# Bringing a column block back from DRAM as two half loads, each issued behind the next half block's store

## The chip, the cores and the metric

The kernel runs on one core of a Trainium2 chip. The metric is the device time of one execution in microseconds. Three runs of the kernel before took 485.42, 486.91 and 487.61 us; their median is 486.91 us. The profile shows one further execution.

## The reference

The reference is a graph layer followed by a mixture of eight experts, on 2048 nodes of 256 features. Cut to what matters:

```python
row, col = src, dst                       # 67584 edges, sorted by dst
gathered = edge_weight[:, None] * layernorm(x)[col]
x = x + segment_sum(gathered, row, num_segments=2048) + node_vec1
# experts, on x after a second layer norm xn:
top_p, top_idx = top_k(softmax(xn_in @ Wr + br), 2)
y_e = gelu((xn * ln_g[e] + ln_b[e]) @ W1[e] + b1[e]) @ W2[e] + b2[e]
x = x + weighted sum of the two chosen y_e
```

Only the first half is touched by the change: the sum over edges, which the kernel turns into a product of a 2048 x 2048 matrix A (a row for each src, a column for each dst, the edge weight as its entry) with the normalised nodes.

## The kernel before, in words

**Building A.** The columns of A are built in 16 column blocks of 128 destinations, and each block in two halves of 64 columns, so there are 32 half blocks, n = 0 to 31 (`NH`, the loop at L513). For a half block VectorE makes three tiles of ones and zeros: `hl` (the low seven bits of src, L328), `eq` (the high bits and the column of a pair, L335) and `hr` (eq times the weight, in three bf16 parts, L343). TensorE multiplies them, 96 small matmuls in `make_cols` (L367), ScalarE copies the result from PSUM to the SBUF tile `ar` (L370, two copies), and SyncE's queue stores `ar` to a DRAM tile `ad` (L371, 512 KB in rows of 512 bytes). The store is a transposition: partition (j, b) of `ar` goes to row 8m + j of `ad`, so that a column of A is a row of `ad`. Half h of a block fills rows 64h to 64h + 63.

**Using A.** When both halves of block cb are stored, one load (L374, 1 MB) brings `ad` back as the tile `ac`, 128 columns on 128 partitions. `dense` (L376 to L385) multiplies a few column blocks (a group of `GROUPS`: blocks 0-2, 3-6, 7-10, 11-13, 14-15) by the normalised nodes `xn` for two of the sixteen row blocks; VectorE adds the result to `acc` (L388), or, up to n = 16, ScalarE stages it and GpSimd's queue adds it by DMA (L396).

**The order.** In this part of the program the order on every engine is written out by hand (`manual_schedule` with all engines). In step n VectorE makes the tiles of half block n + 1 while TensorE runs `make_cols(n)`; from n = 8 on a `dense` follows it: group 0 in n = 8 to 15, group 1 in n = 16 to 23, group 2 in n = 24 to 31, eight pairs of row blocks each. Every fourth half block needs a new window of 128 x 128 edges (GpSimd's indirect DMAs, L242), whose keys VectorE prepares and TensorE transposes (L309). After the loop the first five pairs of group 3 and one of group 4 follow (L599 to L603), then the rest of the dense work and the expert part.

**Queues and buffers.** SyncE's queue issues its DMAs in program order. A load of `ac` waits there until the stores that it reads have landed, and everything behind it in that queue waits too. The behind-lying instructions in step n are the stores of the next half blocks and, at n = 12, two stores of zeros (L588, L590); behind the last load are the experts' weights (L988 to L991). `ar` has three buffers (`rowsp`), `hr` and `hl` two each, `ad` four; the tiles `ac` lie in two pools (`cols_0` with three buffers, `cols_1` with five), so that block 11 takes the buffer of block 3, which the last `dense` of group 1 frees.

Of the kernel before, what the change touches and what calls it, by code (L numbers as in the profile page):

```python
# [22 lines left out]
P = 128  # L23
# [4 lines left out]
def kernel(  # L28
# [30 lines left out]
    nc = tc.nc  # L59
# [170 lines left out]
    def count_before(q):  # L230
        sign = find.tile([P, RUN_0], BF16, name="sign")
        nc.scalar.activation(sign[:, :runs[q].shape[1]], runs[q], AF.Sign, bias=colp[:, q:q + 1],
                             scale=-1.0, accum_out=at[:, q:q + 1])
# [44 lines left out]
    def keys_of(q):  # L278
        b_i, f = low_key(q)
        nc.vector.tensor_tensor(f[:, 1, :], cls[q], b_i, OP.add)  # L280
        return f
# [33 lines left out]
    def next_part(q, i):  # L315

        k2, w2, rest = parts[q]
        r = prep.tile([P, P], F32, name=f"r{i}")
        nc.vector.tensor_tensor(r, rest, w2[:, :, i - 1, 0], OP.subtract)
        nc.scalar.copy(w2[:, :, i, :], r[:, :, None].to_broadcast([P, P, 2]))  # L320
        parts[q] = (k2, w2, r)

    def make_hl(n, hl=None, m=slice(0, GH)):


        k2, g = parts[n // 4][0], n % 4
        hl = hotl.tile([P, GH, P], BF16, name="hl") if hl is None else hl
        nc.vector.tensor_tensor(hl.rearrange("p g (n t) -> p g n t", t=2)[:, m],  # L328
                                two(k2[:, 0], g, P)[:, m], pair(P)[:, m], OP.is_equal)
        return hl  # L330

    def make_eq(n):
        k2, g = parts[n // 4][0], n % 4
        eq = hotr.tile([P, GH, RK], BF16, name="eq")
        nc.vector.tensor_tensor(eq.rearrange("p g (n t) -> p g n t", t=2),  # L335
                                two(k2[:, 1], g, RK), pair(RK), OP.is_equal)
        return eq

    def make_hr(n, eq):
        w2, g = parts[n // 4][1], n % 4  # L340
        hr = hotr.tile([P, GH, 3, RK], BF16, name="hr")
        w = w2[:, g * GH:(g + 1) * GH].rearrange("p g i t -> p (g i) t")
        nc.vector.tensor_tensor(  # L343
            hr.rearrange("p g i (n t) -> p (g i) n t", t=2),
            eq[:, :, None, :].to_broadcast([P, GH, 3, RK]),
            w[:, :, None, :].to_broadcast([P, GH * 3, RK // 2, 2]), OP.mult)
        return hr
# [5 lines left out]
    def make_cols(n, hl, hr):  # L353


        cb, h = n // 2, n % 2
        if h == 0:
            ads[cb] = dram.tile([P, NB, P], F32, name="ad", bufs=CB)
        ad_v = ads[cb].rearrange("(m j) b r -> (j b) m r", m=GB // QP)
        ar = rowsp.tile([P, GH // QP, P], F32, name="ar")  # L360
        for m0 in range(0, GH // QP, 4):
            pa = ps_a.tile([P, 4, P], F32, name="pa")
            for m in range(4):
                for i in range(3):
                    for j in range(QP):
                        g = (m0 + m) * QP + j
                        nc.tensor.matmul(pa[j * RK:(j + 1) * RK, m, :], hr[:, g, i, :],  # L367
                                         hl[:, g, :], start=(i == 0), stop=(i == 2),
                                         tile_position=(0, j * RK))
            nc.scalar.copy(ar[:, m0:m0 + 4, :], pa)  # L370
        nc.sync.dma_start(ad_v[:, h * GH // QP:(h + 1) * GH // QP, :], ar)  # L371
        if h == 1:
            acs[cb] = (cols_0 if cb in GROUPS[0] or 8 <= cb < 11 else cols_1).tile([P, NB, P], F32, name="ac")
            nc.sync.dma_start(acs[cb], ads[cb])  # L374

    def dense(blocks, b, between={}):  # L376

# [9 lines left out]
    def add(b, pa):  # L387
        nc.vector.tensor_add(acc[:, b:b + 2, :], acc[:, b:b + 2, :], pa[:, :, :DX])  # L388
# [9 lines left out]
    ads, acs = {}, {}  # L398
    ET = mybir.EngineType
    ALL = {ET.DVE, ET.Pool, ET.PE, ET.Activation, ET.SP}  # L400
    with tc.manual_schedule(engines=ALL):
# [8 lines left out]
        def center_router():  # L410
            nc.vector.memset(wc[:, :, NE:], 1.0)
            nc.vector.scalar_tensor_tensor(
                wc[:, :, :NE], tr[:, None, nt:nt + NE].to_broadcast([P, KD, NE]), -1.0 / D, wr_sb,
                op0=OP.mult, op1=OP.add)
# [90 lines left out]
        NH = 2 * NB  # L505
# [7 lines left out]
        for n in range(NH):  # L513
            q = n // 4
            f = None
            new = q + 1 if n > 4 and n % 4 == 2 and q + 1 < GQ else None
            if n + 1 < NH:
                hl = make_hl(n + 1) if n else hl_1
                if n == 1:
                    center_router()  # L520
                if n == 3:
                    next_part(1, 2)
                if n == 2:
                    fq = 1
                    f = keys_of(1)
                if new is not None:
                    next_part(new, 1)
                hots[n + 1] = hl, make_hr(n + 1, make_eq(n + 1))
                if new is not None:
                    next_part(new, 2)  # L530
            if n % 4 == 0 and q + 2 < GQ:
                count_before(q + 2)
            if n % 4 == 0 and q and q + 1 < GQ:
                fq = q + 1
                f = keys_of(fq)
            elif n % 4 == 1 and q + 2 < GQ:
                get_win(q + 2)
                if q + 4 < GQ:
                    get_run(q + 4)
            if n in (5, 8, 11, 14):  # L540
                b = 4 * (n // 3 - 1)
                scales_x(slice(b, b + 4))
            if n in (7, 10, 12, 14):
                b = {7: 0, 10: 4, 12: 8, 14: 12}[n]
                weigh_n(slice(b, b + 4))
            for p in late:
                (add_apart if n <= NB else add)(*p)
            late = []
            make_cols(n, *hots.pop(n))
            g, k = divmod(n - NB // 2, NB // 2)  # L550
            if g >= 0:
                late.append(dense(GROUPS[g], 2 * k))
            if n == 0:

                tr = ps_k.tile([P, 3, P], F32, name="pk").rearrange("p a b -> p (a b)")
                nt = NE * KH + 2 * NE * KD + NB
                cols = consts.tile([P, nt], F32, name="cols")
                o = 0
                for rows in (b1_rows, g_rows, be_rows, nv_rows):
                    m = rows.shape[0]  # L560
                    nc.tensor.transpose(tr[:, o:o + m], rows, ident[:m, :m])
                    o += m
                for k in range(KD):
                    nc.tensor.matmul(tr[:, nt:nt + NE], ones, wr_sb[:, k, :], start=(k == 0),
                                     stop=(k == KD - 1))
                nc.scalar.copy(cols, tr[:, :nt])
                nv_c = cols[:, NE * (KH + 2 * KD):]
            if n % 4 == 3 and q + 2 < GQ:
                scale_dst(q + 2)
            if 1 <= n < 9:  # L570
                weigh_x(n - 1)
            if n < 8:
                turn_x(n)
            if n == 1:
                scale_dst(1)
                sort_cols()
            if f is not None:
                turn_keys(fq, f)
            if n == 2:
                next_part(1, 1)  # L580
            for m, work, j in X_WORK:
                if m == n:
                    work(j)
            if n == 12:

                less_m = small.tile([P, NB], F32, name="less_m", bufs=1)
                nc.vector.tensor_tensor(less_m, less, nv_c, OP.subtract)
                nc.sync.dma_start(xr_d[N:, :].rearrange("(t p) c -> p t c", p=P),  # L588
                                  none[:, None, :].to_broadcast([P, TT, RW]))
                nc.sync.dma_start(y_d[N:, :].rearrange("(t p) d -> p t d", p=P),  # L590
                                  none[:, None, :D].to_broadcast([P, TT, D]))
            if n == NH - 3:
                used = small.tile([P, 1], F32, name="used", bufs=1)
                nc.vector.tensor_reduce(used, used_q, AX.X, OP.add)
                used_i = small.tile([1, 1], I32, name="used_i", bufs=1)
                pu = ps_k.tile([P, 3, P], F32, name="pk")[:, 0, :1]
                nc.tensor.matmul(pu, ones, used, start=True, stop=True)
                nc.vector.tensor_copy(used_i, pu[0:1, :])
        for p in range(NA // 2):  # L599
            late.append(dense(GROUPS[3], 2 * p))  # L600
            add(*late.pop(0))
# [722 lines left out]
```

## Time and profile before

| | |
|---|---|
| median of three runs | 486.91 us |
| the profiled execution | 489.3 us |
| its span on the core | 487.4 us |
| TensorE busy, share of the span | 446.5 us, 92% |
| VectorE busy | 268.8 us, 55% |
| stores `ad` | 32 of 512 KB, 6.8 us from issue to landing (median) |
| loads `ac` | 16 of 1024 KB, 6.1 us from issue to landing (median) |
| mean granted TensorE clock | 0.978 |

The edge part lies in the first 192 us of the span or so; the loads `ac` are issued from 29.4 to 193.4 us. VectorE's busy share over the whole kernel says little: in the forty slices of the page it is nine tenths or more from the second slice to the twelfth, which is most of the edge part, and low after it. A time in the working below is a start in the span unless it is called a duration. "Landing" is the time at which a DMA's semaphore says that all of its data are there.

### The profile page before, as it was taken

To read this page: it belongs to the slowest core of one execution; us is meant where nothing else is said; L and a number is where in the kernel's file an instruction comes from. 1 tells how busy PE (TensorE), PEld (TensorE's weight loads), DVE (VectorE), ACT (ScalarE), POOL (GpSimd) and SP (SyncE) were. 2 spreads that over 40 slices of the span, in tenths; PEclk is the share of its full clock that TensorE was granted. 3 is DMA by queue.
4 is the path that set the end of the run, shared out by engine and by line. 5 is a ranking of instruction groups with operands and counts; after the bars stand their busy time and mean duration, and the time that the engine had idled before them with its cause. 6 is when DMAs were issued, how large, how long until landed. Compare 5 with 4: busy or idle time off the path is not lost. (4 is left out here: it accounts for less than half of the span.)

```text
span 487.4 us, 12242 instructions
## 1 busy us (share of the span) xinstructions
PE 446.5 (92%) x5040; PEld 384.1 (79%) x5040; DVE 268.8 (55%) x558; ACT 199.3 (41%) x496; POOL 174.3 (36%) x141
## 2 busy tenths in 40 slices
PE   1588898889996999999999999999999999999895
PEld 0477787667885888888988888888888888879784
DVE  5999999999997975248772312334333212210011
ACT  2568759652432211056772233332334332324320
POOL 5561636653220000002744433554343444222223
PEclk9987799999998999999999999999999999999999
DMA  3678769998768866994629997899999676642331
GB/s 99 235 186 243 232 183 265 265 234 227 198 192 244 254 192 186 344 373 138 122 86 270 323 272 220 223 350 365 354 325 287 183 223 196 174 103 26 100 130 43
DMA packets 88372, 105.58 MB, mean 217 GB/s; under 512 B 9920, under 2 KB 77616, under 8 KB 86192
## 3 DMA queue, kind: packets, MB, share of 16 engines
q1 hardware_dynamic: 79072, 88.95, 58.1%
q0 software_dynamic: 9200, 15.67, 14.4%
q8 instruction: 44, 0.72, 0.6%
q14 instruction: 24, 0.20, 0.1%
q10 hardware_dynamic: 32, 0.04, 0.0%
HBM read 75.11 MB, written 29.47 MB: 215 GB/s over the span
## 5 line engine op out<-in xcount | busy, mean ns | idle before, releaser
L1115 PE MATMUL py<-w,hT 128*128 128x256 f32 x544 | 120.4, 380 | 0.0
L1068 PE MATMUL ph<-xeT,w 128*128 128x256 f32 (+1 forms) x544 | 115.1, 368 | 3.1 <-PEq L1278 1.3
L1070 ACT ACTIVATE hT<-ph,ec 128x256 f32<-128x256 f32 (+1 forms) x136 | 61.9, 460 | 123.9 <-PE ph L1068 69.7
L1115 PEld LDWEIGHTS py<-w,hT 128*128 128x128 f32 x544 | 102.4, 191 | 13.0
L1068 PEld LDWEIGHTS ph<-xeT,w 128*128 128x128 f32 x544 | 98.1, 191 | 16.5 <-issue 3.0
L383 PE MATMUL py<-xn_lo,ac 128*128 128x264 f32 x352 | 86.8, 399 | 5.6 <-DMA ac<-ad 5.6
L1123 POOL DMA_INDIRECT y_d<-ys,to_i x30 | 48.2, 1607 | 112.5 <-DVE ys L1118 80.2
L383 PEld LDWEIGHTS py<-xn_lo,ac 128*128 128x128 f32 x352 | 65.8, 193 | 18.9 <-DMA ac<-ad 6.4
L328 DVE TENSOR_TENSOR hl<-k,iota_b 128x4096 bf16<-128x4096 bf16 (+1 forms) x33 | 73.3, 2220 | 2.5 <-PE pa L367 1.4
L367 PE MATMUL pa<-hl,hr 128*32 128x128 bf16 x3072 | 56.2, 234 | 12.4 <-DVE hr L343 6.6
L367 PEld LDWEIGHTS <-hr 128*32 128x32 bf16 x3072 | 49.1, 104 | 22.6 <-issue 10.8
L1118 DVE SCALAR_TENSOR_TENSOR ys<-py,wt,b2w 128x256 f32<-128x256 f32 x34 | 16.3, 483 | 79.6 <-PE py L1115 76.4
L343 DVE TENSOR_TENSOR hr<-eq,w 128x3072 bf16<-128x3072 bf16 x32 | 56.3, 1758 | 1.9 <-DVE eq L335 0.5
L1042 DVE TENSOR_SCALAR xeT<-px,ec 128x256 f32<-128x256 f32 (+1 forms) x36 | 17.4, 525 | 64.5 <-PE px L1030 64.5
L370 ACT COPY ar<-pa 128x512 f32<-128x512 f32 x64 | 35.4, 593 | 39.0 <-PE pa L367 21.7
L995 POOL DMA_INDIRECT xs<-xr_d,to_i x32 | 33.4, 1045 | 15.2 <-DVE ys L1118 5.6
L242 POOL DMA_INDIRECT win_s<-in_src,at_i x8 | 15.9, 1989 | 60.3 <-DVE at_i L238 45.8
L383 PE MATMUL py<-xn_hi,ac 128*128 128x264 f32 x160 | 36.5, 388 | 0.3 <-PEq L613 0.3
L383 PEld LDWEIGHTS py<-xn_hi,ac 128*128 128x128 f32 x160 | 30.2, 190 | 5.6 <-PEq L613 0.7
L388 DVE TENSOR_TENSOR acc<-acc,py 128x528 f32<-128x528 f32 x29 | 20.3, 701 | 20.9 <-PE py L383 20.7
L1057 ACT ACTIVATE b2w<-b,wt 128x256 f32<-128x256 f32 x36 | 16.3, 500 | 25.7 <-DVE wt L1055 25.7
L335 DVE TENSOR_TENSOR eq<-k,iota_b 128x1024 bf16<-128x1024 bf16 x32 | 21.9, 684 | 0.0
(224 smaller groups left out, 358.7 us busy)
## 6 DMA issues: line engine op xcount, KB each, us to landing
w<-in_L_ffn_W SPq DMA_DIRECT2D x40, 1024.0 KB, 9.2
ad<-ar SPq DMA_DIRECT2D x32, 512.0 KB, 6.8
ac<-ad SPq DMA_DIRECT2D x16, 1024.0 KB, 6.1
b<-in_L_ffn_b SPq DMA_DIRECT2D x20, 128.0 KB, 9.2
acc<-st POOLq DMA_DIRECT2D x8, 264.0 KB, 8.0
acc<-in_x SPq DMA_DIRECT2D x4, 512.0 KB, 4.5
out<-y_d SPq DMA_DIRECT2D x4, 512.0 KB, 4.6
xr_d<-rec SPq DMA_DIRECT2D x1, 1300.0 KB
```

The costliest lines, as they stand in the source:

```text
L328: nc.vector.tensor_tensor(hl.rearrange("p g (n t) -> p g n t", t=2)[:, m], two(k2[:, 0], g, P)[:, m], pair(P)[:, m], OP.is_equal)
L335: nc.vector.tensor_tensor(eq.rearrange("p g (n t) -> p g n t", t=2), two(k2[:, 1], g, RK), pair(RK), OP.is_equal)
L343: nc.vector.tensor_tensor(hr.rearrange("p g i (n t) -> p (g i) n t", t=2), eq[:, :, None, :].to_broadcast([P, GH, 3, RK]), w[:, :, None, : ...
L367: nc.tensor.matmul(pa[j * RK:(j + 1) * RK, m, :], hr[:, g, i, :], hl[:, g, :], start=(i == 0), stop=(i == 2), tile_position=(0, j * RK))
L370: nc.scalar.copy(ar[:, m0:m0 + 4, :], pa)
L383: nc.tensor.matmul(pa[:, i, :DX], acs[c][:, b + i, :], xn(c), start=(c == blocks[0]), stop=(c == blocks[-1]))
L388: nc.vector.tensor_add(acc[:, b:b + 2, :], acc[:, b:b + 2, :], pa[:, :, :DX])
L995: nc.gpsimd.indirect_dma_start(out=(sets[s.set][0] if into is None else into)[:, t, cols], out_offset=None, in_=(xr_d if rows is None else ...
L1068: nc.tensor.matmul(ph, w1[:, k, c * P:(c + 1) * P], xeT[:, k, :], start=(k == 0), stop=(k == KD - 1))
L1070: nc.scalar.activation(hT[:, c, :s.n * P], ph, AF.Gelu, bias=ec[:, c:c + 1], scale=1.0)
L1115: nc.tensor.matmul(py, hT[:, c, t * P:(t + 1) * P], w2[:, c, :], start=(c == 0), stop=(c == KH - 1))
L1123: st = nc.gpsimd.indirect_dma_start(out=y_d[:, :], out_offset=bass.IndirectOffsetOnAxis(ap=tos[s.to][:, t:t + 1], axis=0), in_=ys, in_offs ...
```

## The change

The one load of a block becomes two, each of 64 of its rows onto 64 partitions (512 KB). A half load is no longer issued behind the store that it reads, but one half block later: at the end of `make_cols(n)`, behind the store of half block n, the half n - 1 is loaded. The last half is loaded after the loop. The buffer of `ac` is taken when the first half of a block is loaded, which is at the same place of the program where the whole block was loaded before.

```diff
         nc.sync.dma_start(ad_v[:, h * GH // QP:(h + 1) * GH // QP, :], ar)
-        if h == 1:
+        if n > 0:
+            get_half(n - 1)
+
+    def get_half(n):
+        cb, h = n // 2, n % 2
+        if h == 0:
             acs[cb] = (cols_0 if cb in GROUPS[0] or 8 <= cb < 11 else cols_1).tile([P, NB, P], F32, name="ac")
-            nc.sync.dma_start(acs[cb], ads[cb])
+        rows = slice(h * P // 2, (h + 1) * P // 2)
+        nc.sync.dma_start(acs[cb][rows], ads[cb][rows])
...
                 nc.vector.tensor_copy(used_i, pu[0:1, :])
+        get_half(NH - 1)
         for p in range(NA // 2):
             late.append(dense(GROUPS[3], 2 * p))
             add(*late.pop(0))
```

Nothing moves on TensorE, VectorE, ScalarE or GpSimd; SyncE's queue gets 16 more DMAs and the new order: store n, half load n - 1, store n + 1, half load n, and so on.

## The prediction

> **What bounds the kernel now.** I read the slices of the page first, then what SyncE's queue and TensorE wait for, then the timeline around each wait of TensorE. The slices:
>
> ```profile
> PE   1588898889996999999999999999999999999895
> DVE  5999999999997975248772312334333212210011
> PEclk9987799999998999999999999999999999999999
> DMA  3678769998768866994629997899999676642331
> ```
>
> VectorE is full up to slice 12 (146 us) and sets the pace at first; TensorE is full from slice 10 on, but for slice 13 (146 to 158 us), where its clock dips too. The waits of SyncE's queue over the span (total, times, longest):
>
> ```profile
> SPq L374 <- DMA ad<-ar: 98.2, 16, 15.4
> SPq L371 <- ACT ar L370: 51.9, 18, 11.2
> ```
>
> Each load sits about 6 us behind the store just ahead of it, and the next stores sit behind the load. TensorE's waits from 85 to 240 us, the three longest:
>
> ```profile
> PE py L383 <- DMA ac<-ad: 5.6, 2, 3.8
> PE pa L367 <- issue: 2.1, 1, 2.1
> PE pa L367 <- ACT ar L370: 0.6, 1, 0.6
> ```
>
> Where these fall, from the timeline (start, duration, engine, instruction; the brackets are the idle time ahead):
>
> ```profile
> 103.82 2.49 PE L383 MATMUL py<-xn_lo,ac 128*128 128x264 f32 x10 [1.76 <-DMA ac<-ad]
> 106.57 1.52 PE L367 MATMUL pa<-hl,hr 128*32 128x128 bf16 x96
> 112.58 1.08 ACT L370 COPY ar<-pa 128x512 f32<-128x512 f32 x2 [4.22 <-DMA ad<-ar]
> 140.61 1.76 DVE L343 TENSOR_TENSOR hr<-eq,w 128x3072 bf16<-128x3072 bf16 x1 [0.48 <-DVE eq L335]
> 144.86 0.33 SPq L374 DMA_DIRECT2D ac<-ad  x1
> 151.04 4.04 PE L383 MATMUL py<-xn_lo,ac 128*128 128x264 f32 x10 [3.84 <-DMA ac<-ad]
> 155.47 1.52 PE L367 MATMUL pa<-hl,hr 128*32 128x128 bf16 x96
> ```
>
> TensorE is without a gap from 103.82 to 147.2 us, except 0.58 us at 112.6; from 151.04 it is full to the end of the edge part and, with waits of about 3 us in all, through the experts to 470 us. So from 92 us on, what TensorE waits for is what the end waits for. (The 2.1 us "issue" lie ahead of that, in n = 14, and have no releaser.) Three gaps are due to the column blocks' way through DRAM:
> - 1.76 us at 102: the first `dense` of group 1 waits for block 6, whose load left the queue at 97.36.
> - 0.58 us at 112.6: ScalarE waits for an `ar` buffer, since two stores were held behind that load and landed 14.8 and 15.9 us after issue; TensorE waits for ScalarE.
> - 3.84 us at 147.2: the first `dense` of group 2 waits for block 10, loaded at 144.86, landed at 151.0. The lag never closed: from 114 to 145 the loads left at 114.24, 123.89, 134.24 and 144.86, each as soon as the two stores ahead had landed, about 10 us apart.
>
> After the third gap the matmuls are slow. Ten matmuls of `dense` and three transposes took 155.47 - 151.04 = 4.43 us; the same work took 106.57 - 103.82 = 2.75 us after the first gap. The granted clock says why: 0.76, then 0.50, then 0.74 in the stretches between 151.04 and 156, 1.00 before. This gap costs 3.84 + 1.68 = 5.52 us. All three: 1.76 + 0.58 + 5.52 = 7.86 us.
>
> **The change, part by part.** *The wait behind the own store goes.* A half load is issued behind the next half's store, 5.2 to 5.5 us after its own; a store that isn't held lands in 4 to 7 us, so the queue waits 0 to 2 us where it waited 6. Stores leave when ScalarE has copied. Behind the load in the queue stand the next store and, in n = 12, the two stores of zeros (1.95 and 1.42 us to issue); all come earlier or as before.
>
> *16 more issues* at 0.33 us each, 5.3 us on a queue that mostly waits: nothing. The last two loads put about 0.4 us ahead of the experts' weights (193.8 us), which move forward by the gain and are not waited for by TensorE: nothing; uncovered, 0.4 us.
>
> *A block is whole later in program order.* Its second half leaves behind one more store. For block 10: ScalarE ends its copy of half 22 at 138.1 (its step is held by VectorE's keys, so this doesn't move), store 22 leaves at 138.2, half load 21 at 138.6. The load for half 22 onwards must wait for block 3's buffer as before.
>
> *The price of a half load.* No row shows a load onto 64 partitions. The whole load lands in 6.1 us. The nearest row is the load of x in pieces of 512 KB, 4.5 us on 128 partitions: the lower end, with no gain below it, since half the bytes take no less than the shortest store of as many (3.2 us), which would buy 1.3 us more only where nothing waits. The upper end is 6.1 us, a half as slow as a whole. Here the Trainium skill speaks against the change: "SBUF — State Buffer", section "Door 1: The DMA port swizzle", gives 64 partitions half of the ports, 196 GB/s against 328 on 128 at 1 MiB; "DMA: Bandwidth & Descriptors", "Rules for kernel authors", says not to split a transfer into partition halves. By the row a half load costs the engines half of a whole one and the change is free; by the rule it costs 328/196 = 1.67 times that. I estimate by the rule, since only it speaks of partitions: landing 6.1 x 0.5 x 1.67 = 5.1 us alone.
>
> Is there room on the DMA engines? From 114 to 145 they are 0.76 busy, 7.9 us for a block. In the weights' stretch (206 to 212 us) they moved 381 GB/s at 1.07 busy, so a whole load costs 1.05 MB / 381 x 1.07 = 2.9 us, and the rest 5.0. By the rule: 5.0 + 2.9 x 1.67 = 9.9 us for a block, while TensorE takes 2 x 5.2 = 10.4 to 10.7. It fits, barely.
>
> *Where the gaps go.* Block 10: half load 21, issued at 138.6, stands behind 512 KB of store 22 (about 2 us of engine time: 5.0 for two stores and some windows), so it lands at 138.6 + 2 + 5.1 = 145.7. It is wanted at 147.2, less what the earlier gaps gave. Third gap: nearly all gone, -5.2 us (0.3 left). Block 6: store 13 stands behind the zeros and landed about 97 before, so half load 13 leaves at 97 with store 14 half done ahead of it and lands at 97 + 1 + 5.1 = 103.1 against 103.8: -0.7 us. `ar`: store 15 stands behind 512 KB of load in place of 1 MB and lands well before 111.8: -0.6 us. Sum: -6.5 us.
>
> *What is late next is VectorE.* At n = 24 its `hr` is ready at 142.37 (141.9 without a 0.48 us wait for TensorE), TensorE takes it at 144.14: 2.2 us of slack, enough for the first two gaps. From there to the `hr` of n = 31 (186.69) VectorE waited 1.66 + 1.22 + 3.35 us for TensorE; without them and the 0.48 it is ready at 180.0, and TensorE can start its last half block at about 180.4 against 187.05. So no more than 6.6 us can be had. Since both engines then run close together, I take 0.8 us off for handing over: -5.7 us. The experts' part behind hangs on TensorE and moves with it. The profiled execution would be 489.3 - 5.7 = 483.6; it lies 2.4 us above the median, so the forecast is 486.9 - 5.7 = 481.2 us.
>
> **The rivals.**
> *A: half loads fill the DMA engines (slower).* If a half load costs as much as a whole one, a block costs 5.0 + 5.8 = 10.8 us of DMA, over TensorE's 10.4 to 10.7. It decides from about 1.9 times up (5.0 + 2.9 x 1.9 = 10.5). Place: 95 to 114 us, where the engines are 0.96 busy already with windows and the accumulating DMAs; 2.9 us more for a block puts block 6 some 5 us late, and the backlog doesn't drain, so block 10 stays as late as now. +3.3 at the first gap, about +1 in the later steps: 491. For it: the slices 90 to 110 us. Against: the rule's own figure is 1.67.
> *B: the wait only moves (no change).* Block 6 is later by 2 to 4 us, since its second half stands behind a store and collides with the accumulations (99 to 103 us), but the pipelined queue catches up before n = 24: +3 - 0.6 - 5.2 + handing over = 484 to 487; I take 485.5.
> *C: nothing.* The loads still wait for a store that lands late (15 us at worst), and block 10 comes at 150: 486.9. Against it: the 15 us came of the queue's own hold-up.
>
> **How the numbers follow.** The likeliest 0.56, with its own range 479.8 (a little over VectorE's limit) to 483.5 (half load 21 lands 2 us late); B 0.18; C 0.07; A 0.19. Faster by over 0.5% (about what a measurement of this kernel can tell from no change), below 484.5: 0.56 + a quarter of B = 0.61. Slower, above 489.3: A = 0.19. Within: 0.20. The range: 479.8 up to 490.5, which leaves out the further part of A.
>
> **What would show it.** SyncE's wait for the stores from 98 us to under 40; the stores leave evenly, about 5 us apart, not in pairs. No gap of TensorE near 147 and no clock dip behind it; the gap for block 6 near 1 us. The engines' share from 114 to 145 us rises from 0.76 to about 0.95 if the rule holds, and stays near 0.76 if half loads cost half. `add` of n = 24 to 31 no longer waits for TensorE. I would be wrong if half load 13 landed after 106, if a half load alone took over 6 us, or if VectorE had more work to wait for than the 6.6 us show.

## The result, and the profile after

The changed kernel takes 492.3 us (median of 18 runs, 489.25 to 498.38) against 489.63 us for the kernel before (18 runs, 485.42 to 495.41): 1.0077 times as long, with an interval of 1.0052 to 1.0102. The ratio, like those below, leaves out executions in a second, slower state (one of the 18 of the changed kernel here), so it is not the quotient of the two medians. The forecast was 481.2 us; the change makes the kernel a little slower. The profiled execution took 489.25 us with a span of 487.5 us, the lowest of the 18, so it is nearly equal to the profiled execution of before (489.3 and 487.4 us). These two traces show a gain and a loss that cancel. The further 3 us of the changed kernel's median are not in them.

The slices of the changed kernel:

```profile
PE   1588899769999999999999999999999999999895
DVE  5999999996999985248772212333333212210011
PEclk9995789999999999999999999999999999999999
DMA  3788879999968697995529997799999686642241
```

The dip of TensorE has moved from slice 13 to slices 8 and 9 (85 to 110 us), and VectorE, which was full up to slice 12, now has a hole in slice 10. The waits of SyncE's queue:

```profile
SPq L371 <- ACT ar L370: 80.5, 21, 11.1
...
SPq L380 <- DMA ad<-ar: 34.6, 16, 8.5
```

The wait of the loads for the stores fell from 98.2 to 34.6 us, as the prediction said (under 40). The queue now mostly waits for ScalarE, that is for work. But one wait of 8.5 us is left. TensorE's waits from 85 to 245 us:

```profile
PE py L389 <- DMA ac<-ad: 4.1, 1, 4.1
PE pa L367 <- issue: 3.8, 3, 1.8
```

Two waits for a column block have become one. Where it is, the timeline says, first around block 6, then around block 10:

```profile
101.37 1.52 PE L367 MATMUL pa<-hl,hr 128*32 128x128 bf16 x96
102.82 1.60 PE L389 MATMUL py<-xn_lo,ac 128*128 128x264 f32 x6
108.53 4.12 PE L389 MATMUL py<-xn_lo,ac 128*128 128x264 f32 x10 [4.11 <-DMA ac<-ad]
...
112.91 1.52 PE L367 MATMUL pa<-hl,hr 128*32 128x128 bf16 x96
...
149.75 1.52 PE L367 MATMUL pa<-hl,hr 128*32 128x128 bf16 x96
151.21 3.83 PE L389 MATMUL py<-xn_lo,ac 128*128 128x264 f32 x16
```

Block 10 no longer holds TensorE: the first `dense` of group 2, now at 151.21, runs without a bracket and at full speed, sixteen matmuls in 3.83 us. But block 6 comes at 108.5 instead of 103.8. The six matmuls on blocks 3 to 5 end at 104.42, then TensorE stands for 4.11 us, and the ten behind run at a granted clock of 0.62 (108.5 to 113.0 us), 4.12 us instead of 2.49.

The account of the two traces closes. Start of `make_cols(17)`: 106.57 before, 112.91 after, 6.34 us later. TensorE was already 2.37 us later at `make_cols(16)` (99.00, now 101.37); the gap is 4.11 instead of 1.76, 2.35 more; the slow clock costs 4.38 - 2.75 = 1.63, taken over the ten matmuls and three transposes. Sum 6.35. The first two terms are one: TensorE has to wait for block 6 in any case, which comes at 108.53 instead of 103.82, 4.71 us later; had TensorE been there earlier, the gap would have been longer by as much. On the other side, the 5.52 us at block 10 and the 0.58 us for `ar` are gone, 6.10. The difference is +0.24, and the last half block, `make_cols(31)`, starts at 187.24 instead of 187.05.

Why block 6 is late is to be read in SyncE's queue (start and duration of each issue; L371 stores, L380 loads, L594 and L596 the zeros):

```profile
79.69 0.36 SPq L371 DMA_DIRECT2D ad<-ar  x1
80.73 0.45 SPq L380 DMA_DIRECT2D ac<-ad  x1
83.44 0.36 SPq L371 DMA_DIRECT2D ad<-ar  x1
91.12 0.45 SPq L380 DMA_DIRECT2D ac<-ad  x1
91.62 1.24 SPq L594 DMA_DIRECT2D xr_d<-none  x1
92.91 0.46 SPq L596 DMA_DIRECT2D y_d<-none  x1
93.42 0.55 SPq L371 DMA_DIRECT2D ad<-ar  x1
95.69 0.45 SPq L380 DMA_DIRECT2D ac<-ad  x1
96.47 0.36 SPq L371 DMA_DIRECT2D ad<-ar  x1
100.66 0.45 SPq L380 DMA_DIRECT2D ac<-ad  x1
```

Store 11 left at 79.69 and landed at 91.1, 11.4 us later, among the accumulating DMAs and the windows (the engines' share from 80 to 90 us is 1.07). Half load 11 waited for it until 91.12, for 7.2 us (the longest wait, 8.5 us, is that of half load 15 at 115.31, behind store 15). Behind it in the queue stood the zeros and store 13, whose data ScalarE had ready at 89.3; store 13 left at 93.42 and landed at 100.6. Half load 13, the second half of block 6, left at 100.66 and landed at 108.5, 7.9 us later. The early part of the queue is as crowded as before, since the accumulating DMAs and the windows have not moved, and now the block needs one store more in front of it.

### The profile page after: what moved, and what is told of

Its sections match the earlier page's. It is cut to its first block, busy times and chain, and to the rows that moved or that the text cites. A ratio compares the mean times of both kernels' runs of the same rounds, so it can differ in the third digit from the quotient of the medians.

```text
span 487.5 us, 12272 instructions
## 1 busy us (share of the span) xinstructions
PE 448.0 (92%) x5040; PEld 385.9 (79%) x5040; DVE 268.8 (55%) x558; ACT 199.7 (41%) x496; POOL 169.8 (35%) x141
## 5 line engine op out<-in xcount | busy, mean ns | idle before, releaser
L389 PE MATMUL py<-xn_lo,ac 128*128 128x264 f32 x352 | 87.8, 403 | 4.1 <-DMA ac<-ad 4.1
L389 PEld LDWEIGHTS py<-xn_lo,ac 128*128 128x128 f32 x352 | 66.8, 195 | 17.7 <-issue 4.7
L242 POOL DMA_INDIRECT win_s<-in_src,at_i x8 | 14.0, 1750 | 68.5 <-DVE at_i L238 51.0
L394 DVE TENSOR_TENSOR acc<-acc,py 128x528 f32<-128x528 f32 x29 | 20.2, 700 | 22.5 <-PE py L389 22.4
## 6 DMA issues: line engine op xcount, KB each, us to landing
b<-in_L_ffn_b SPq DMA_DIRECT2D x20, 128.0 KB, 9.6
```

What stands on the lines that cost most here:

```text
L389: nc.tensor.matmul(pa[:, i, :DX], acs[c][:, b + i, :], xn(c), start=(c == blocks[0]), stop=(c == blocks[-1]))
```

## The experiments

The ratios are to the kernel before on the same chip, with their intervals. The chips differ: the kernel before took 488.8 us on one of them, and 501.2 to 501.4 us on the three others (the chip of the result above is not on record), so times of different chips are not compared. Two theories stand:

- **A, the place in the queue**: putting a load one store further back makes the early blocks late, where stores land late, and this eats what the later blocks gain.
- **B, the partitions**: a half load onto 64 partitions costs more of the DMA engines than half of a whole load.

### Which part of the change costs

**defer_whole.** The whole 1 MB load, behind the store of the next half block; no halves.

```diff
-        if h == 1:
...
-            nc.sync.dma_start(acs[cb], ads[cb])
+        if n > 0 and n % 2 == 0:
+            get_block(n // 2 - 1)
...
+        nc.sync.dma_start(acs[cb], ads[cb])
```

> The whole block loaded in one piece onto 128 partitions, but behind the next half block's store, where the changed kernel loads its second half: the delay without the split. Theory A (it is the place in the queue: block 6 comes too late for the first product of group 1, because its load stands behind a store that lands late in the jam of 80 to 110 us): the gap of TensorE for block 6 is 3 to 5 us as in the changed kernel, the gap for block 10 is gone or under 1 us, ratio 1.004 to 1.01. Theory B (half loads onto 64 partitions cost the DMA engines more): without them the jam is as before, block 6 comes with a gap of at most 2 us, and the ratio is 0.987 to 0.995.

Measured: 506.79 us, 1.0121 (1.0067 to 1.0175). Block 10 holds nothing, block 6 comes with a gap of 6.89 us, block 2 with 2.06. That is the direction of A, with more of it than A had said (a gap of 3 to 5 us, 1.004 to 1.01). Whole loads moved back cost as well, so the halves are not needed for a loss.

**defer_by_rows, rows_2** (the same kernel on two chips). The same place, but two loads of 64 rows onto 64 partitions, back to back; the edit is shown against defer_whole.

```diff
-        nc.sync.dma_start(acs[cb], ads[cb])
+        for h in range(2):
+            rows = slice(h * P // 2, (h + 1) * P // 2)
+            nc.sync.dma_start(acs[cb][rows], ads[cb][rows])
```

> As the whole deferred load, but as two loads right behind one another, each of 64 rows onto 64 partitions. Theory A: like the whole deferred load within 0.3%. Theory B: slower than the deferred load in two column halves by at least 3 us, and the DMA engines' busy share from 114 to 145 us is 0.85 or more against 0.76.

> The deferred load as two loads of 64 rows onto 64 partitions again, in the hope of a chip on which the kernel before takes its usual 485 to 490 us (it took 501 on the first chip). Theory B (64 partitions are dear everywhere): slower than the two column halves by 1% or more, TensorE's waits for its issue in the edge part 10 us or more. Theory A (the place in the queue alone decides on a usual chip): within 0.4% of the column halves, ratio about 1.01 for both.

**defer_by_cols, cols_2.** The same number of loads and bytes, each of 8 row blocks onto all 128 partitions; shown against defer_by_rows.

```diff
-            rows = slice(h * P // 2, (h + 1) * P // 2)
-            nc.sync.dma_start(acs[cb][rows], ads[cb][rows])
+            bs = slice(h * NB // 2, (h + 1) * NB // 2)
+            nc.sync.dma_start(acs[cb][:, bs], ads[cb][:, bs])
```

> As the whole deferred load, but as two loads right behind one another, each of 8 of the 16 row blocks onto all 128 partitions: as many DMAs of the same size as with rows, only the partitions differ. Theory A: within 0.3% of the deferred load in two row halves. Theory B: as fast as the whole deferred load, and 3 us or more faster than the one in row halves.

> The deferred load as two loads of eight row blocks onto all 128 partitions again, beside the one above. Theory A: ratio 1.005 to 1.012, as the row halves. Theory B: ratio 1.0 to 1.008 and 1% or more under the row halves.

Measured: by rows 525.54 us, 1.0358 (1.0271 to 1.0444), and 526.26, 1.0406 (1.0339 to 1.0473); by row blocks 509.69, 1.0218 (1.0163 to 1.0274), and 510.48, 1.0212 (1.0173 to 1.0251). Two loads instead of one cost about 1%, which B had put at nothing (the two intervals just overlap); the pieces by rows, onto 64 partitions, cost 1.4% and 1.9% more. That is B's direction; what else differs in this pair is said at spread_cols.

**split_own.** Half loads, each right behind its own store: the halves without the delay.

```diff
-        if n > 0:
-            get_half(n - 1)
+        get_half(n)
```

> Half loads onto 64 partitions, each right behind its own store: the split without the delay. SyncE's queue then waits for each store. Theory A: block 6 is whole about when it was before, the gap for block 6 is 1 to 3 us and that for block 10 is 2 to 4 us, ratio 0.997 to 1.005. Theory B: the half loads cost as in the changed kernel, ratio 1.006 or more, and the engines' busy share from 114 to 145 us rises to 0.85 or more.

Measured: 537.71 us, 1.0771 (1.0713 to 1.0828). SyncE's waits in this kernel:

```profile
SPq L379 <- DMA ad<-ar: 158.8, 30, 12.0
```

Thirty waits instead of sixteen, 158.8 us instead of 98.2: every store now has a load waiting behind it that holds the next store. The engines' share from 114 to 145 us is 0.74, so it is the queue that is full here and not the engines. This is on B's side (1.006 or more), but B's own sign, a share of 0.85 or more, is not there. Half loads without the delay are far worse than with it.

### Whether the early jam is what the change loses to

**after_again, after_third.** The changed kernel again, on two chips, of which the first is like that of the result (488.8 us before) and the second one of the slower three.

> The changed kernel once more, on this chip, for a second profile and a ratio beside the partial ones. Theory A (block 6 comes too late since its half load stands behind stores that land late in the jam): a gap of TensorE for block 6 of 3 to 6 us with a clock dip, none for block 10; ratio 1.005 to 1.01 on any chip. Theory B (half loads onto 64 partitions hold up the DMA engines, and with them TensorE's instruction fetch, seen as TensorE waiting for nothing but its issue in the midst of a run of small matmuls): these waits are 8 us or more in the edge part where the kernel before has about 4, and the ratio on a chip as slow as the one of the first four runs is 1.02 or more.

> The changed kernel again, so that it stands on one chip beside the three others of this job. Theory A (block 6 late, since half load 13 stands behind the zeros and store 13): gap for block 6 of 3 us or more with a clock dip, ratio 1.005 to 1.012 on a usual chip, 1.01 to 1.02 on one where the kernel before takes 500 us. Theory B (64 partitions dear in themselves): the same ratio; the two part in the runs beside it.

Measured: 491.56 us, 1.007 (1.003 to 1.011), with a gap of 5.58 us at block 6 and none at block 10; and 504.01 us, 1.0065 (1.0033 to 1.0097), with this line:

```profile
110.85 4.74 PE L389 MATMUL py<-xn_lo,ac 128*128 128x264 f32 x10 [6.52 <-DMA ac<-ad]
```

The loss is the same in all three measurements, also on the slower chip, where A had expected 1.01 to 1.02. All three traces have the gap at block 6: 4.11, 5.58 and 6.52 us, each with a slow clock behind it. In after_again `make_cols(31)` starts at 188.02 us, 0.97 later than in the trace of before, and the span is 1.1 us longer: there the loss lies in the edge part.

**after_noacc, before_noacc.** Both kernels without the eight accumulating DMAs; the part of the sum that they bring is left out, which changes the routing and makes the experts' part longer in both. Only the pair is to be compared.

```diff
-        nc.gpsimd.dma_start(acc[:, b:b + 2, :], st, accum_op=OP.add)
```

> The changed kernel without the eight accumulating DMAs of group 0 (the sum of its column blocks is left out of the output): the jam is lighter. To be read against the kernel before without them. Theory A: block 6 comes in time (gap under 1.5 us) and the changed order is then faster than the old one by 3 us or more. Theory B: the changed order stays slower by 2 us or more, since the half loads are as dear as before.

> The kernel before without the eight accumulating DMAs of group 0 (their sum is left out of the output), the control of the run above. Theory A: the gap for block 6 is gone, that for block 10 is under 2 us, ratio 0.988 to 0.995. Theory B: the same; the two differ in the pair's difference only.

Measured: 501.73 us, 1.0283 (1.0249 to 1.0317), and 500.25, 1.0252 (1.0218 to 1.0287). The changed kernel's line:

```profile
102.66 2.46 PE L389 MATMUL py<-xn_lo,ac 128*128 128x264 f32 x10 [0.48 <-DMA ac<-ad]
```

Without the accumulating DMAs its gap at block 6 falls to 0.48 us (1.31 us are left at block 2), and the clock stays full. But the kernel before has no gap for a column block at all then, not even at block 10: its lag of the loads began in the same jam. The edge parts end almost alike (`make_cols(31)` at 181.30 and 181.74). So most of the gap goes with the accumulating DMAs; and without them there is nothing for the change to gain, where A had expected 3 us or more. How full the engines are is not what decides: from 80 to 90 us their share is still 1.05 in the changed kernel without the accumulating DMAs (0.66 in the kernel before without them), yet half load 11 leaves 6.6 us after store 11 instead of 11.4.

**after_zeros, before_zeros.** Both kernels with the two stores of zeros at n = 20 instead of n = 12, out of the jam.

```diff
             if n == 12:
...
                 nc.vector.tensor_tensor(less_m, less, nv_c, OP.subtract)
+            if n == 20:
                 nc.sync.dma_start(xr_d[N:, :].rearrange("(t p) c -> p t c", p=P),
```

> The changed kernel with the two stores of zeros moved from step 12 to step 20, out of the way of store 13 and half load 13. Theory A: half load 13 comes 2 to 4 us earlier, the gap for block 6 falls from 4 to 6 us to under 2 and the ratio from 1.007 to 0.992 to 1.000. Theory B: the half loads are as dear as before, ratio 1.003 or more.

> The kernel before with the zeros moved from step 12 to step 20, the control for the changed kernel with the zeros moved. Theory A: the gap for block 6 shrinks from 1.8 to under 1 us, the later load for block 10 comes earlier too: ratio 0.990 to 0.998. If it gains as much as moving the zeros gained the changed kernel (0.5 to 1% of the time), the change itself is no worse and no better for them; if it gains nothing, the zeros hurt only the changed order, as theory A has it.

Measured: 503.31 us, 1.0019 (0.9987 to 1.005), and 500.81, 0.9989 (0.9958 to 1.0019). First the changed kernel at block 6:

```profile
109.76 2.46 PE L389 MATMUL py<-xn_lo,ac 128*128 128x264 f32 x10 [0.97 <-DMA ac<-ad]
```

then the kernel before at block 10:

```profile
151.91 2.49 PE L383 MATMUL py<-xn_lo,ac 128*128 128x264 f32 x10 [3.28 <-DMA ac<-ad]
```

With the zeros away the gap of the changed kernel is 0.97 us, and of its loss (1.0065 to 1.007) about a quarter is left. The kernel before gains only 0.1% by the same move, within the error, and still waits 3.28 us for block 10; A had expected a little more (0.990 to 0.998). Why the zeros cost the changed kernel more is argued, not shown: they stand ahead of store 13 in both kernels, but only in the changed one does store 14 stand between it and the load that needs it. The 1.0019 lies between what A (up to 1.000) and B (1.003 or more) had expected. The two ratios of the changed kernel come from two chips and their intervals overlap, so the size of this part, 0.5%, is not certain; that the gap shrinks is.

**defer_late, defer_late_zeros.** Whole loads; blocks 0 to 7 behind their own store as before, blocks 8 to 15 behind the next half's store. The expectations count the blocks one too high. The second kernel has the zeros at n = 20 too.

```diff
-        if h == 1:
...
-            nc.sync.dma_start(acs[cb], ads[cb])
+        late_cb = NB // 2
+        if n % 2 == 1 and n // 2 < late_cb:
+            get_block(n // 2)
+        if n % 2 == 0 and n // 2 > late_cb:
+            get_block(n // 2 - 1)
```

> Whole loads onto 128 partitions; blocks 0 to 8 behind their own store as before, blocks 9 to 15 behind the next half block's store. Theory A: the early jam is left as it was, block 6 as late as before (gap 1 to 3 us), the gap for block 10 falls to under 1 us: ratio 0.988 to 0.995. Theory B: the same, since no load is split; if the ratio is 1.00 or more, the place in the queue is no gain even without the split and without the jam, and both theories miss something.

> The version that the runs so far point to: whole loads, blocks from 9 on behind the next half block's store, and the zeros in step 20. Theory A: both gaps go, for block 6 and for block 10: ratio 0.986 to 0.993 (the deferral alone had 0.9965). Theory B: likewise no split; it says nothing else.

Measured: 486.72 us, 0.9965 (0.9939 to 0.9992), on the chip on which the changed kernel took 491.56; and 498.98 us, 0.9915 (0.9887 to 0.9943). The delay of whole loads does bring a gain where it is applied only to the blocks that come after the jam, while applied to all of them it lost 1.2% (defer_whole, on another chip). The gain is 0.35%, less than A had expected (0.988 to 0.995) and less than a third of the 1.2% forecast for the change. With the zeros out of the way as well it is 0.85%, on the chip on which the changed kernel with the zeros moved had 1.0019. In the trace of this second kernel (an execution of 500.78 us, above its median) block 6 has no gap; one of 2.09 us is left at the start of group 2:

```profile
156.80 2.49 PE L389 MATMUL py<-xn_lo,ac 128*128 128x264 f32 x10 [2.09 <-DMA ac<-ad]
```

A reservation: in the trace of defer_late, whose order up to block 7 is that of before, block 6 came with a gap of 4.48 us, where the trace of before has 1.76. The jam varies from one execution to the next, so a single gap's size is not a measure; the ratios are.

### Whether 64 partitions are dear

**spread_rows, spread_cols.** Two half loads at the same places, each half a block later than in the change (behind store n, part n - 2), once 64 rows onto 64 partitions, once 8 row blocks onto 128.

```diff
-        if n > 0:
-            get_half(n - 1)
+        if n > 1:
+            get_part(n - 2)
...
+        rows = slice(h * P // 2, (h + 1) * P // 2)         # spread_rows
+        nc.sync.dma_start(acs[cb][rows], ads[cb][rows])
+        bs = slice(h * NB // 2, (h + 1) * NB // 2)         # spread_cols
+        nc.sync.dma_start(acs[cb][:, bs], ads[cb][:, bs])
```

> Each half load of 64 rows one half block later than in the changed kernel, one behind each store: a partner for the run with column halves, with the same places in the queue. Block 6 comes about 5 us later than in the changed kernel in both, so both are slow. Theory B: slower than the column halves by 1% or more. Theory A: within 0.4% of them.

> The same places in the queue, but each half load is eight row blocks onto all 128 partitions. Theory B: faster than the row halves by 1% or more, and TensorE's waits for its issue in the edge part at least 4 us fewer. Theory A: within 0.4%.

Measured: 520.67 us, 1.0409 (1.0347 to 1.0472), and 501.39, 0.9992 (0.996 to 1.0024). Both had been expected to be slow; the second is not. The two kernels differ in which half a load takes, and the difference is 4.2%. TensorE's waits from 20 to 200 us, by rows:

```profile
PE py L389 <- DMA ac<-ad: 10.0, 3, 5.3
PE pa L367 <- issue: 9.9, 16, 2.4
```

and by row blocks:

```profile
PE pa L367 <- issue: 4.6, 8, 1.3
...
PE py L389 <- DMA ac<-ad: 1.7, 1, 1.7
```

So the halves by rows are dearer at this place, by far more than I had allowed. Yet the changed kernel, also with 64 partitions, was only 0.65% slower on the same chip: the price differs with the place of the load.

Two things more are to be read from spread_cols, at block 6:

```profile
100.87 0.33 SPq L380 DMA_DIRECT2D ac<-ad  x1
106.20 2.49 PE L389 MATMUL py<-xn_lo,ac 128*128 128x264 f32 x10 [1.74 <-DMA ac<-ad]
```

First, the pairs differ in more than the partitions. The first product of a group takes row blocks 0 and 1, and these lie in the first part by row blocks; by the semaphores of the trace TensorE waits here for that part alone, while the second, issued at 101.72, lands at 115.1 and is first waited for at 128.0. Halves by rows are both needed at once. So the 1.4%, 1.9% and 4.2% hold the price of the partitions and this head start together, and no run parts them.

Second, the landing. This part stands behind store 14, where half load 13 stands in the change, with as many bytes, and TensorE has it 5.3 us after its issue. Half load 13 left at 100.66, 100.40 and 102.66 us in the three traces of the changed kernel, and TensorE had it 7.9, 8.3 and 8.2 us later. The engines were as full (a share of 1.07 from 95 to 114 us here and in after_third, 1.09 in after). By this one trace, then, about 3 us of the gap at block 6 go with the 64 partitions, and without them the place in the queue leaves a gap as it was before the change, 1.74 us. The ratio of 0.9992 has the head start in it as well.

## Why the prediction was wrong, point by point

**Right.** The loads' wait for the stores fell to 34.6 us. The gap at block 10 went with its clock dip, 5.52 us, and the `ar` gap, 0.58; the forecast for both was 5.2 + 0.6. Sixteen more issues cost nothing that the traces show. Block 10 is the step on which most of the forecast gain rested.

**The step that failed** is "half load 13 leaves at 97 ... and lands at 97 + 1 + 5.1 = 103.1 ... -0.7 us". It left at 100.66 and landed at 108.5, beyond the 106 that the prediction named as the point at which it would be wrong. The lateness of 5.4 us has two terms. It left 3.7 us late, since I let store 13 land "about 97" as in the trace of before, while it now stood behind half load 11, which waited 7.2 us for store 11, and behind the zeros. I had written that "a store that isn't held lands in 4 to 7 us", although rival A itself called the engines 0.96 busy from 95 to 114 us (by the trace of before it is 0.87 there); from 80 to 90 us they were 1.09 busy before the change and 1.07 after it, and store 11 took 11.4. And it landed 1.8 us slower, 7.9 instead of 1 + 5.1. Onto 128 partitions, at the same place in spread_cols, a piece of as many bytes took 5.3 us, so by that trace the second term is a price of the partitions that the estimate of 5.1 had too low for this stretch.

A term was left out besides: the gap costs clock too. I had priced the dip at block 10 and did not ask whether a gap that moves to block 6 brings its own. It brought 1.63 us. With the two, the forecast of -0.7 became -0.7 + 5.4 + 1.63, the +6.34 at `make_cols(17)`, and the forecast sum of -6.5, with 6.10 gained elsewhere instead of 5.8, became +0.2.

The 2.37 us by which TensorE was late ahead of the gap are not a further cost, since half load 13 left when store 13 had landed, and the data of store 13 had lain ready for 4.1 us. 1.06 of them were there at the start of `make_cols` at 84.58 (before: 83.52), most of them from VectorE, whose `hl` at 32.88 us comes 0.79 later than before; in defer_late, with the order of before up to there, it comes 0.65 later. The rest are longer waits of TensorE that have no releaser, 1.76 + 1.69 us instead of 2.13 in that stretch. The two other traces of the changed kernel have one such wait there, of 1.96 and 1.59 us, so neither part has to come from the change.

**The rival that came true** is B, "the wait only moves", with its place, block 6, and its cause, a second half behind one more store amid the accumulations. Its price was too low: "+3" against 6.34, since block 6 came 4.7 us later and not 2 to 4, and because of the clock. In the two profiled executions it cancels the gain to 0.2 us. Rival A had the right place, "some 5 us late", and its 491 is nearest to the median, but in part by luck: its block 10 "as late as now" did not come.

**Partitions.** A half load landed 6.4 us after its issue in the median; a whole one, with twice the bytes, took 6.1 before. With the 1 us that the prediction had added to its 5.1 for a store beside the load this nearly fits; in the jam it does not (7.9). Packets of SyncE's DMAs took 61.0% of 487.5 us after, against 58.1% of 487.4 before: 14.2 us, or 0.89 us for a block. On the estimate of 2.9 us for a whole load this is 1.31 times. By the row (512 KB onto 128 partitions at half the price) it should have been 1.0; by the estimate from the Trainium skill, "SBUF — State Buffer", "Door 1: The DMA port swizzle", 328/196 = 1.67, which I took. The paired kernels give 1.48 (rows_2 against cols_2: 58.0% of 521.8 less 55.4% of 506.0 us) and 1.33 (spread_rows against spread_cols: 57.4% of 519.7 less 57.5% of 492.2 us). All of these count packet time, with the waiting of packets in crowded stretches in it. The direction of the rule is right and, summed over the kernel, its size too large here; the engines' share from 114 to 145 us rose to 0.85, between the 0.76 and 0.95 of the two readings. So from 114 us on there was room, as forecast. In the jam there was none: from 90 to 130 us the share rose from 0.86 to 1.06.

**The starting point.** I took 2.4 us off since the profiled execution lay that far above the median of three runs. By the 18 runs the median is 489.63 and the profiled execution lies on it; by my own steps the forecast should have been 483.9. These 2.7 us are a quarter of the miss of 11.1; the rest is the step above and what stays open.

**What stays open.** The ratio is 1.0077 while the two traces are equal; three traces of the changed kernel show gaps at block 6 of 4.11 to 6.52 us, and with the zeros moved the ratio is nearer to 1, but the loss of the median was not followed term by term. How much of it is the partitions and how much the place is not separated in full: spread_cols speaks for the partitions, after_zeros for the place, and halves by row blocks can't all be loaded at the change's own places, since each needs both stores of a block. Why whole loads moved back lose (defer_whole), where the halves of spread_cols do not, no run shows. And the cause of the waits described next is not known.

## What to carry to other kernels

When a wait is taken off a queue by moving the waiting DMA further back, price it at each place where the queue passes through a crowded stretch, with the landing times of that stretch and not with the median: here whole loads moved back gained at the blocks behind the jam (0.9965 with the early blocks left alone) and lost when moved everywhere (1.0121). When a gap moves instead of going, ask what clock the work behind it will have. And if a load must be cut, cut it so that each piece still fills all 128 partitions and the first holds what is needed first: together, in the same places, this was worth 1.4% to 4.2% of the kernel here.

## What the hardware showed that was not expected

**TensorE waits with no releaser while the DMA engines are half idle.** In spread_rows `make_cols` breaks into handfuls of matmuls about 0.73 us apart, with nothing in the profile that TensorE waits for:

```profile
101.99 0.26 PE L367 MATMUL pa<-hl,hr 128*32 128x128 bf16 x4 [0.50 <-issue]
102.74 0.25 PE L367 MATMUL pa<-hl,hr 128*32 128x128 bf16 x3 [0.48 <-issue]
103.47 0.26 PE L367 MATMUL pa<-hl,hr 128*32 128x128 bf16 x4 [0.48 <-issue]
```

In the edge part of this kernel VectorE waits 22.4 us for these matmuls, 7.5 us at the longest. The engines' share from 102 to 107 us is 0.62, and from 73 to 78 us, where the same happens, 0.27, so the DMA engines are not full when it occurs. Both places lie on the windows' indirect DMAs. All kernels show some of this wait in the edge part (2.4 to 8.3 us with loads onto 128 partitions, in the change's places or in split_own), the kernels whose halves of 64 partitions go back to back or half a block later most (19.1 in defer_by_rows, 13.3 in rows_2, 9.9 in spread_rows). It could be the supply of instructions, which the page counts among the core's DMA queues (q8, 44 packets), but no run took that away, and it wasn't settled.

**The length of a gap alone does not tell what clock follows it.** Behind every gap for a column block of 3.54 us or more, up to 8.26 us, the clock dipped; where ten matmuls followed, they took 3.49 to 4.77 us instead of 2.49, so the dip cost 1.0 to 2.3 us. Below that it went both ways. Gaps of 1.74, 1.76, 2.09 and 3.28 us were followed by the full clock. But in defer_whole a gap of 2.06 us was not:

```profile
66.98 3.74 PE L386 MATMUL py<-xn_lo,ac 128*128 128x264 f32 x8 [2.06 <-DMA ac<-ad]
```

These eight matmuls take 2.02 us at full clock. The granted clock was 1.00 from 61 to 66.9 us, ahead of this gap and in it, and 0.54 behind it, from 66.98 to 70.7 us. Behind a gap of 2.85 us in defer_by_rows ten matmuls took 3.65 us. What decides below 3.5 us, these traces do not show.
